# Softmax denominators in a transformer block: which engine sums the last two key tiles

## The chip, the core and the metric

The kernel runs on one core of a Trainium2 chip. The metric is the device time of one execution in microseconds (us). A core has five engines that run their own instruction lists in order and wait for each other by semaphores: TensorE (PE in the profile; its weight loads are PEld), VectorE (DVE), ScalarE (ACT), GpSimd (POOL) and SyncE (SP), which here issues DMA transfers. TensorE multiplies matrices held in the on-chip memory SBUF and leaves the results in PSUM, which has eight banks of 128 x 512 fp32.

## The reference

One block of a transformer, for one sequence of 2048 tokens of width 1024: a modulation from a vector c, layer norm, causal attention with 32 query heads and 8 key and value heads of width 32, an output product with a gate, layer norm again, and a routed low-rank layer. Cut to what matters here:

```python
mod = (_silu(L0_c) @ L0_wmod).reshape(L0_c.shape[0], 6, 1, -1)
...
h = _layernorm(x, axis=-1) * (1 + ca) + sa
q = (x @ Wq).reshape(b, t, N_HEADS, HEAD_DIM).transpose(0, 2, 1, 3)
...
q = _apply_rope(q, cos, sin)
k = _apply_rope(k, cos, sin)
scores = jnp.einsum('bhqd,bhkd->bhqk', q, k_h) / math.sqrt(HEAD_DIM)
causal = jnp.triu(jnp.ones((t, t), dtype=bool), k=1)
scores = jnp.where(causal[None, None], jnp.finfo(scores.dtype).min, scores)
attn = jax.nn.softmax(scores, axis=-1)
ctx = jnp.einsum('bhqk,bhkd->bhqd', attn, v_h)
...
x = x + ga * _L0_attn_ref(h, L0_attn_Wq, L0_attn_Wk, L0_attn_Wv, L0_attn_Wo)
h = _layernorm(x, axis=-1) * (1 + cb) + sb
x = x + gb * _L0_ffn_ref(h, L0_ffn_route_w, L0_ffn_A, L0_ffn_Bw)
```

The softmax needs, for every query and head, the sum over all keys of the exponentials of the scores. These sums are the denominators of the title.

## The kernel before

**Steps and tiles.** Attention is cut into 32 steps, four blocks of 512 queries times eight groups of four heads. A step in block qb has 4 (qb + 1) key tiles of 128 keys: 4, 8, 12 and 16. For one key tile, `weights` (L1472) computes the scores of four heads, 128 keys by 512 queries each, into four PSUM banks, and ScalarE writes their exponentials into a buffer `et` of 128 x 4 x 512 fp32. The row maxima that are subtracted are found beforehand by separate products (`maxima_units`, L1402), reduced on VectorE, cast on GpSimd (`split_maxima`, L1437 to L1447) and turned by TensorE into rows (`shift_rows`, L1449). Of the last four tiles of each step the mask removes queries: tile nk - 2 holds only the last 256 of the 512 queries, tile nk - 1 only the last 128 (`offset`, L1469).

**What is done with a tile of exponentials.** `weighted_sum` (L1503) multiplies it with the values on TensorE, into one bank for the step. `accumulate` (L1516) adds it on GpSimd to an SBUF buffer `acc` of the same shape: tile 1 starts it as the sum of tiles 0 and 1, and tiles 2 to nk - 3 follow. The last two tiles are left out of `acc`. `denominators` (L1528) then sums over the keys by products with a matrix of ones: first `acc`, 512 queries wide, then the last two tiles, 256 and 128 wide, all into one bank `pd`. ScalarE copies it to `rd`, VectorE inverts it in four pieces (`invert`), and GpSimd multiplies the step's output by it (`divide`, L1545). In the last step VectorE does the adds in place of GpSimd.

**Buffers.** There are four `et` buffers and one `acc`. An `et` is free when TensorE's product with the values and its add, or for the last two tiles the product with ones, are done. The next step's first add can start once the product with ones has read `acc`.

**Order.** All instructions are issued in an order that `plan_order` (L97) finds at build time. It searches over small units: maxima (M), scores (S), weighted sums with their adds (P), denominators (D), the shift rows (R), pieces of the projections and of the output product (F), and the tail of each token tile (T). It keeps a model of when each engine, bank and buffer will be free, with a cost per unit written by hand; `sums` (L235) holds the model of the adds and `shares` (L258) that of the denominators. The best order is then issued as it stands (L1614 to L1645). So when the model's costs change, the whole order changes. A denominators unit may be chosen once all weighted sums of its step are issued (L346), and the next step's add of tile 1 only after it (L344).

**Two more users of GpSimd.** `rotary` (L834) applies the position rotation of queries and keys, partly on GpSimd (L844, L845), with a table `cs` that is loaded for each projection into a single buffer (L825, L826, issued on SyncE) and has one half multiplied by a sign on ScalarE (L832). The output product adds its gated result to the residual on GpSimd (L1112).

Of the kernel before, what the change touches and what calls it, by code (L numbers as in the profile page):

```python
# [25 lines left out]
QB = 512  # L26
# [51 lines left out]
TO_ENGINE, TO_PE, BETWEEN = 0.25, 0.2, 0.15  # L78
# [18 lines left out]
def plan_order(parts, trail, steps, ahead, starts, tiles, ends, rates, gates):  # L97
# [36 lines left out]
    last_step = len(steps) - 1  # L134
# [4 lines left out]
    def start(s, form, ready):  # L139

        old = s[FORM]
        if form == "Rb":
            price = 0.145 if old != "R" else 0.03
            form = "R"
        elif form == "R":
            price = 0.225 if old != "R" else 0.03
        elif form == "C":
            price = 0.11 if old == "R" else 0.16 if old == "W" else 0.02
        else:
            price = 0.11 if old == "R" else 0.16 if old == "C" else 0.06  # L150
        s[FORM] = form
        at = s[PE] + price
        return ready if ready > at else at

    def use(s, engine, us, after):
        t = s[engine]
        t = (after if after > t else t) + us
        s[engine] = t
        return t + 0.09

    def take(s, n):

        s[GOT] = tuple(bank for _, bank in s[FREE][:n])
        ready, s[FREE] = s[FREE][n - 1][0], s[FREE][n:]
        return ready

    def give(s, *banks):
        s[FREE] = tuple(sorted(s[FREE] + banks))

    def free_et(s, at, n):  # L170
        s[ETS] = s[ETS] + (at + BETWEEN,) * n

    def flush(s):
        while s[LATER]:
            divide(s)
# [56 lines left out]
    def et_ready(s, i):  # L232
        return s[READY][i - s[SCORED] + 4]

    def sums(s):  # L235
        i = s[SUMMED]
        n, kc = tiles[i]
        nk = 4 * (steps[n][0] + 1)
        width = QB - max(0, kc * P - steps[n][0] * QB)
        ready = et_ready(s, i)  # L240
        at = ready + TO_PE
        if kc == 0:
            at = max(at, take(s, 1))
            s[SUM_BANK] = s[GOT][0]
        s[PE] = start(s, "C", at) + 0.00167 * width
        s[WORK] += 0.00167 * width
        if kc == nk - 1:
            give(s, (use(s, ACT, 0.5, s[PE] + TO_ENGINE) + TO_PE, s[SUM_BANK]))
        adder, us = (DVE, 0.0043) if n == last_step else (POOL, 0.00875)
        if kc == 1:  # L250
            s[ACC] = use(s, adder, us * QB, max(ready + BETWEEN, s[ACC_FREE]))
            free_et(s, max(s[ACC], s[PE]), 2)
        elif 1 < kc < nk - 2:
            s[ACC] = use(s, adder, us * width, ready + BETWEEN)
            free_et(s, max(s[ACC], s[PE]), 1)
        s[SUMMED] += 1

    def shares(s):  # L258
        flush(s)
        n = s[SHARED]  # L260
        ready = max(take(s, 1), s[ACC] + TO_PE, et_ready(s, ends[n] - 1) + TO_PE)
        s[PE] = start(s, "C", ready) + 0.00167 * (QB + 384)
        s[WORK] += 0.00167 * (QB + 384)
        s[ACC_FREE] = s[PE] + TO_ENGINE
        free_et(s, s[PE], 2)
        s[RD] = use(s, ACT, 0.5, s[PE] + TO_ENGINE)
        give(s, (s[RD] + TO_PE, s[GOT][0]))
        s[LATER] = 5
        s[SHARED] += 1
# [57 lines left out]
    def choices(s):  # L327
# [14 lines left out]
        if s[SUMMED] < s[SCORED]:  # L342
            n, kc = tiles[s[SUMMED]]
            if not (s[SHARED] < n and kc == 1) and s[FILL] >= sums_need[s[SUMMED] > 0]:  # L344
                found.append((et_ready(s, s[SUMMED]) + TO_PE, "P", sums))
        if s[SHARED] < last_step and s[SUMMED] >= ends[s[SHARED]]:  # L346
            found.append((max(one, s[ACC] + TO_PE), "D", shares))
# [25 lines left out]
    s = [0.0] * len(Plan.FIELDS)  # L373
# [24 lines left out]
    while key <= top:  # L398
# [13 lines left out]
        for _, s in sorted(kept.values(), key=lambda k: k[0])[:WIDTH]:  # L412
# [4 lines left out]
            if s[LATER] and s[DVE] < s[PE]:  # L417
                s = list(s)
                divide(s)
            while (  # L420
# [3 lines left out]
                s = list(s)  # L424
                follow(s)
            found = choices(s)
            if not found:

                if s[TRAIL] < s[KNOWN] and not KINDS[trail[s[TRAIL]]][0]:
                    n = tokens_for.get(s[TRAIL], 0)  # L430
                    if n > len(s[TOKENS]):
                        continue
                    s = list(s)
# [30 lines left out]
def adaln_block_kernel(  # L464
# [105 lines left out]
    class Stream:  # L570
        def __init__(self, pool, tag, depth):
            self.pool, self.tag, self.depth = pool, tag, depth
            self.loads, self.tiles = [], []
            self.freed = self.used = 0
# [9 lines left out]
        def take(self, n=1):  # L584
            got = self.tiles[self.used : self.used + n]
            assert len(got) == n
            self.used += n
            return got
# [78 lines left out]
    def bank(name):  # L667
        count[0] += 1
        return psum.tile([P, QB], F32, tag=f"b{chosen.pop(0)}", name=f"{name}_{count[0]}")
# [177 lines left out]
    class Project:  # L847
# [77 lines left out]
        def start(self):  # L925
            self.h_t = one.tile([P, NC, TB], F32, tag="h_t", name=f"h_t_{self.b}")
# [532 lines left out]
    class Attend:  # L1459
        def __init__(self, n):  # L1460
            self.n = n
            self.qb, self.m = steps[n]
            self.nk = 4 * (self.qb + 1)
            self.ets = {}

            last = n == len(steps) - 1
            self.adder = nc.vector if last else nc.gpsimd

        def offset(self, kc):  # L1469
# [46 lines left out]
        def accumulate(self, kc):  # L1516

            off, et = self.offset(kc), self.ets[kc]
            if kc == 1:
                self.acc = one.tile([P, 4, QB], F32, tag="acc", name=f"acc_{self.n}")  # L1520
                first = self.ets[0]
                if off:
                    self.adder.tensor_copy(self.acc[:, :, :off], first[:, :, :off])
                self.adder.tensor_add(self.acc[:, :, off:], first[:, :, off:], et[:, :, off:])  # L1524
            elif 1 < kc < self.nk - 2:
                self.adder.tensor_add(self.acc[:, :, off:], self.acc[:, :, off:], et[:, :, off:])  # L1526

        def denominators(self):  # L1528
            pd = bank(f"pd_{self.n}")
            parts = [(0, self.acc)]  # L1530
            parts += [(self.offset(kc), self.ets[kc]) for kc in (self.nk - 2, self.nk - 1)]
            for i, (off, et) in enumerate(parts):
                for j, rows in groups:
                    nc.tensor.matmul(  # L1534
                        pd[rows, off:], ones_p[:, :HD], et[:, j, off:],
                        start=(i == 0), stop=(i == 2),
                    )
            self.rd = one.tile([P, QB], F32, tag="rd", name=f"rd_{self.n}")
            nc.scalar.copy(self.rd, pd)  # L1539
# [28 lines left out]
    ends = [sum(s.nk for s in attend[: n + 1]) for n in range(len(steps))]  # L1568


    parts, phase_ends, costs, held = [], [0], [], {}
# [12 lines left out]
    for qb in range(NQB):  # L1584
        nk = 4 * (qb + 1)
# [28 lines left out]
    for letter, banks in order:  # L1614
# [8 lines left out]
        i = done_of[letter]  # L1623
        done_of[letter] += 1
        if letter == "M":
            units[i]()
            n = ahead[i][0]
            if i == final[n]:
                split_maxima(n)
        elif letter == "S":  # L1630
            n, kc = tiles[i]
            now[0] = n
            attend[n].weights(kc)
        elif letter == "P":
            n, kc = tiles[i]
# [68 lines left out]
```

## Time and profile before

The median of three runs is 1782.79 us (1782.09 to 1783.23). The profiled execution took 1782.16 us, of which 1780.4 us lie between its first and last instruction (the span); its granted TensorE clock averages 0.996 of full speed.

| stretch (us from the span's start) | TensorE busy | VectorE busy | ScalarE busy | GpSimd busy |
|---|---|---|---|---|
| 157 to 329 (denominators of steps 0 to 7) | 168.12 of 172 | 106.38 | 59.89 | 68.06 |
| 329 to 656 (to step 15) | 324.34 of 327 | 206.34 | 131.40 | 219.50 |
| 656 to 1163 (to step 23) | 503.22 of 507 | 310.25 | 218.00 | 374.47 |
| 1684 to 1780.4 (last step and the end) | 86.99 of 96.4 | 76.96 | 44.77 | 35.70 |

The costliest groups that the change concerns, by shape:

| line, engine | tile and width | count | busy us | mean ns |
|---|---|---|---|---|
| L1526 GpSimd add | acc, 2048 elements per partition | 157 | 713.3 | 4543 |
| L1526 GpSimd add | acc, 1536 elements | 23 | 79.5 | 3455 |
| L1524 GpSimd add | acc from tiles 0 and 1, 2048 elements | 23 | 104.4 | 4541 |
| L1534 TensorE product with ones | acc, 512 columns | 256 | 34.7 | 615 |
| L1534 TensorE product with ones | tile nk - 2, 256 columns | 256 | 20.2 | 387 |
| L1534 TensorE product with ones | tile nk - 1, 128 columns | 256 | 13.2 | 277 |

How to read it: a busy time is the time in which at least one instruction of the group ran. An fp32 product counts as two instructions, and the four heads' products run beside each other in the array and overlap, so their mean is not what one of them costs; that is read from the start of one group of products to the start of the next. GpSimd's and VectorE's instructions don't overlap with others of the same engine.

### The profile page before, as it was taken

To read this page: it belongs to the slowest core of one execution; us is meant where nothing else is said; L and a number is where in the kernel's file an instruction comes from. 1 tells how busy PE (TensorE), PEld (TensorE's weight loads), DVE (VectorE), ACT (ScalarE), POOL (GpSimd) and SP (SyncE) were. 2 spreads that over 40 slices of the span, in tenths; PEclk is the share of its full clock that TensorE was granted. 3 is DMA by queue.
4 is the path that set the end of the run, shared out by engine and by line. 5 is a ranking of instruction groups with operands and counts; after the bars stand their busy time and mean duration, and the time that the engine had idled before them with its cause. 6 is when DMAs were issued, how large, how long until landed. Compare 5 with 4: busy or idle time off the path is not lost.

```text
span 1780.4 us, 55951 instructions
## 1 busy us (share of the span) xinstructions
PE 1747.0 (98%) x25112; PEld 708.9 (40%) x25112; DVE 1094.3 (61%) x2160; ACT 740.0 (42%) x1634; POOL 1185.1 (67%) x568
## 2 busy tenths in 40 slices
PE   7999999999999999999999999999999999999997
PEld 3655555444444333334444343333333333333333
DVE  2455456755755674676475566575566765666497
ACT  1203334344433424455444333454544444455452
POOL 1233343487567649657885866978979778798852
PEclk9999999999999999999999999999999999999999
DMA  9512323212422421131103011101102111110101
GB/s 350 181 30 74 115 80 103 73 50 62 137 73 96 153 87 49 49 102 61 61 26 125 26 49 68 41 37 49 49 25 73 37 61 49 49 49 25 49 13 49
DMA packets 68496, 130.57 MB, mean 73 GB/s; under 512 B 3744, under 2 KB 20768, under 8 KB 68256
## 3 DMA queue, kind: packets, MB, share of 16 engines
q1 hardware_dynamic: 66928, 125.85, 20.5%
q8 instruction: 196, 3.21, 0.8%
q10 hardware_dynamic: 1328, 1.15, 0.2%
q14 instruction: 44, 0.36, 0.1%
HBM read 118.59 MB, written 8.39 MB: 71 GB/s over the span
## 4 chain that ended last, share of the span: by engine, by line
PE 88%; POOL 6%; DVE 2%; issue 2%; DMA 1%; ACT 1%; POOLq 0%; ACTq 0%; DVEq 0%
PE sm L1426 15%; PE po L1508 14%; PE sc L1492 12%; PE pw L675 11%; PE pq L966 11%; PE sc L1479 5%; POOL acc L1526 5%; PE pd L1534 3%; PE pk L675 3%; PE pv L675 2%; PE pa L675 2%; PE open L966 2%; PE pf L675 2%; PE sm L1419 1%; DVE mx L1432 1%
## 5 line engine op out<-in xcount | busy, mean ns | idle before, releaser
L1432 DVE TENSOR_REDUCE mx<-sm 128x1 f32<-128x512 f32 (+3 forms) x1280 | 689.0, 602 | 397.7 <-PE sm L1426 396.2
L1498 ACT ACTIVATE et<-sc 128x512 f32<-128x512 f32 (+3 forms) x1280 | 578.4, 540 | 705.5 <-PE sc L1492 701.3
L1526 POOL TENSOR_TENSOR acc<-acc,et 128x2048 f32<-128x2048 f32 (+1 forms) x180 | 792.8, 4404 | 31.8 <-ACT et L1498 22.8
L1426 PE MATMUL sm<-k_t,q 32*128 32x512 f32 (+3 forms) x3328 | 336.6, 475 | 3.0 <-ACT et L1498 3.0
L1492 PE MATMUL sc<-q,k_t 32*128 32x512 f32 (+3 forms) x2560 | 297.2, 536 | 0.0
L1508 PE MATMUL po<-et,v_sb 128*32 128x512 f32 (+3 forms) x2560 | 294.8, 538 | 0.1
L675 PE MATMUL pw<-w,q 128*32 128x512 f32 x1920 | 238.7, 598 | 0.0
L1524 POOL TENSOR_TENSOR acc<-et,et 128x2048 f32<-128x2048 f32 (+1 forms) x31 | 132.1, 4261 | 98.5 <-ACT et L1498 83.1
L966 PE MATMUL pq<-h_t,w 128*32 128x256 f32 x3072 | 191.9, 384 | 0.0
L1426 PEld LDWEIGHTS sm<-k_t,q 32*128 32x128 f32 x3328 | 139.5, 184 | 116.9 <-issue 43.5
L966 PEld LDWEIGHTS pq<-h_t,w 128*32 128x32 f32 x3072 | 90.5, 110 | 100.6 <-issue 44.8
L1508 PEld LDWEIGHTS po<-et,v_sb 128*32 128x32 f32 x2560 | 59.0, 108 | 175.5 <-issue 152.3
L1543 DVE RECIPROCAL rd<-rd 128x128 f32<-128x128 f32 x128 | 112.4, 919 | 18.9 <-ACT rd L1539 18.8
L1479 PE MATMUL sc<-nt,ones_h 32*128 32x512 bf16 (+3 forms) x1280 | 120.1, 352 | 3.5 <-ACT rd L1539 2.9
L1112 POOL TENSOR_TENSOR x<-ag,x 128x512 f32<-128x512 f32 x40 | 60.9, 1523 | 87.3 <-DVE ag L1111 87.3
L1492 PEld LDWEIGHTS sc<-q,k_t 32*128 32x128 f32 x2560 | 115.5, 185 | 5.8 <-issue 2.1
L1479 PEld LDWEIGHTS <-ones_h 32*128 32x128 bf16 x1280 | 32.9, 91 | 207.6 <-issue 201.5
L844 POOL TENSOR_TENSOR swap_q<-swap_q,cs 128x512 f32<-128x512 f32 x32 | 40.9, 1277 | 105.7 <-DVE swap_q L841 105.7
L675 PEld LDWEIGHTS pw<-w,q 128*32 128x32 f32 x1920 | 50.1, 109 | 129.3 <-issue 110.8
L1547 POOL TENSOR_TENSOR q<-q,rd 128x512 f32<-128x512 f32 x31 | 41.6, 1343 | 67.3 <-DVE rd L1543 49.5
L1111 DVE TENSOR_TENSOR ag<-pw,gate 128x512 f32<-128x512 f32 x40 | 27.5, 687 | 62.5 <-PE pw L675 60.9
L844 POOL TENSOR_TENSOR swap_k<-swap_k,cs 128x512 f32<-128x512 f32 x8 | 10.2, 1276 | 82.7 <-DVE swap_k L841 82.7
(146 smaller groups left out, 1340.0 us busy)
## 6 DMA issues: line engine op xcount, KB each, us to landing
w<-in_wo_dram SPq DMA_DIRECT2D x112, 256.0 KB
w<-in_wmod_dram SPq DMA_DIRECT2D x48, 512.0 KB
w<-in_wq_dram SPq DMA_DIRECT2D x48, 512.0 KB
x<-in_x_dram SPq DMA_DIRECT2D x32, 512.0 KB
out_dram<-x SPq DMA_DIRECT2D x16, 512.0 KB
w<-in_wv_dram SPq DMA_DIRECT2D x12, 512.0 KB
w<-in_wk_dram SPq DMA_DIRECT2D x12, 512.0 KB
wq<-in_wq_dram SPq DMA_DIRECT2D x8, 512.0 KB
```

Source lines behind the costliest of these rows:

```text
L675: nc.tensor.matmul(dst[rows], left[:, rows], right, start=start, stop=stop)
L966: nc.tensor.matmul(ps[j * HD : (j + 1) * HD, a * TB : (a + 1) * TB], self.query_weights(half, k, j * P + h * HD), self.h_t[:, k, :], start ...
L1112: nc.gpsimd.tensor_add(x1[t][:, cols], tmp, x1[t][:, cols])
L1426: nc.tensor.matmul(ps[j][:, a:b], q[rows, t * P : (t + 1) * P], k[rows, kc * QB + a : kc * QB + b], start=not masked, stop=(a, b) == spans ...
L1432: nc.vector.tensor_reduce(mx[:, t, j : j + 1, kc], ps[j][:, :nk], AX.X, ALU.max)
L1479: nc.tensor.matmul(ps[j][:, off:], ones_h[rows, :], nt[rows, off:], start=True, stop=False,)
L1492: nc.tensor.matmul(ps[j][:, off:], k[rows, kc * P : (kc + 1) * P], q[rows, off:], start=False, stop=True,)
L1498: nc.scalar.activation(et[:, j, off:], ps[j][:, off:], AF.Exp, scale=1.0 / math.sqrt(HD))
L1508: nc.tensor.matmul(self.po[rows, off:], v_sb[:, kc, 4 * (self.m // 4) + j, :], et[:, j, off:], start=(kc == 0), stop=(kc == self.nk - 1),)
L1524: self.adder.tensor_add(self.acc[:, :, off:], first[:, :, off:], et[:, :, off:])
L1526: self.adder.tensor_add(self.acc[:, :, off:], self.acc[:, :, off:], et[:, :, off:])
L1543: nc.vector.reciprocal(part, part)
```

## The change

The adder takes the last two tiles as well in all steps but the last, and the product with ones has one part instead of three there. The last step, in which VectorE adds, keeps its three parts. The planner's model is changed in the same way: `sums` counts an add for every tile from 2 on and frees the tile's buffer when it is done, and `shares` waits for the adder alone, costs 512 columns instead of 896 and no longer frees two buffers.

```diff
-        elif 1 < kc < nk - 2:
+        elif 1 < kc < (nk - 2 if n == last_step else nk):
             s[ACC] = use(s, adder, us * width, ready + BETWEEN)
             free_et(s, max(s[ACC], s[PE]), 1)
...
-        ready = max(take(s, 1), s[ACC] + TO_PE, et_ready(s, ends[n] - 1) + TO_PE)
-        s[PE] = start(s, "C", ready) + 0.00167 * (QB + 384)
-        s[WORK] += 0.00167 * (QB + 384)
+        s[PE] = start(s, "C", max(take(s, 1), s[ACC] + TO_PE)) + 0.00167 * QB
+        s[WORK] += 0.00167 * QB
         s[ACC_FREE] = s[PE] + TO_ENGINE
-        free_et(s, s[PE], 2)
...
             last = n == len(steps) - 1
+
+            self.apart = 2 if last else 0
             self.adder = nc.vector if last else nc.gpsimd
...
-            elif 1 < kc < self.nk - 2:
+            elif 1 < kc < self.nk - self.apart:
                 self.adder.tensor_add(self.acc[:, :, off:], self.acc[:, :, off:], et[:, :, off:])
...
             parts = [(0, self.acc)]
-            parts += [(self.offset(kc), self.ets[kc]) for kc in (self.nk - 2, self.nk - 1)]
+            apart = range(self.nk - self.apart, self.nk)
+            parts += [(self.offset(kc), self.ets[kc]) for kc in apart]
             for i, (off, et) in enumerate(parts):
                 for j, rows in groups:
                     nc.tensor.matmul(
                         pd[rows, off:], ones_p[:, :HD], et[:, j, off:],
-                        start=(i == 0), stop=(i == 2),
+                        start=(i == 0), stop=(i == self.apart),
                     )
```

The order of the whole program is planned anew with these costs.

## The prediction

> **What bounds the kernel now.** I read the page's busy shares first, then what TensorE waited for, then the last full block, then single step ends.
>
> ```profile
> PE 1747.0 (98%) x25112; PEld 708.9 (40%) x25112; DVE 1094.3 (61%) x2160; ACT 740.0 (42%) x1634; POOL 1185.1 (67%) x568
> PE 88%; POOL 6%; DVE 2%; issue 2%; DMA 1%; ACT 1%; POOLq 0%; ACTq 0%; DVEq 0%
> ...
> PE mr L781 <- DVE sign L557: 8.9, 1, 8.9
> PE mc L793 <- DVE rows L787: 5.1, 6, 1.4
> PE sm L1426 <- ACT et L1498: 3.0, 1, 3.0
> PE sc L1479 <- ACT rd L1539: 2.9, 1, 2.9
> PE pwh L1174 <- DVE wh L1166: 2.8, 1, 2.8
> ...
> core 0: us, PE busy (x) PEld busy (x) DVE busy (x) ACT busy (x) POOL busy (x), PEclk, DMA share, GB/s
> 1163.00:1684.00 521.00, 519.81 (x6140) 177.34 (x6132) 330.41 (x636) 250.29 (x534) 443.95 (x152) 1.00 0.13 46
> ```
>
> TensorE is busy 1747.0 of 1780.4 us, and the chain of waits is 88% TensorE. What it waits for (us in total, times, longest) is nearly all at the two ends of the run; between 329 and 1733 us its waits come to 6.7 us, of which the 3.0 is the largest. The last row is the stretch from the denominators of step 23 to those of step 30, seven steps: TensorE 519.81 of 521 us, GpSimd 443.95. So work taken from TensorE shortens the run, as long as GpSimd, which is second there at 85%, can take its share without making TensorE wait. The 6% of GpSimd in the chain is no wait of that size: the chain runs through its adds between 1331 and 1373 us, for instance, where TensorE shows no idle time.
>
> **What is removed.** In 31 of 32 steps the denominators' product loses two parts, 256 and 128 columns wide for four heads; the last step keeps them.
>
> ```profile
> 1605.34 3.45 POOL L1526 TENSOR_TENSOR acc<-acc,et 128x1536 f32<-128x1536 f32 x1
> 1605.86 0.79 ACT L1498 ACTIVATE et<-sc 128x128 f32<-128x128 f32 x4 [3.77 <-PE sc L1492]
> 1608.73 1.27 POOL L1112 TENSOR_TENSOR x<-ag,x 128x512 f32<-128x512 f32 x1
> 1612.18 1.07 PE L1534 MATMUL pd<-acc,ones_p 128*32 128x512 f32 x8
> 1613.06 0.83 PE L1534 MATMUL pd<-et,ones_p 128*32 128x256 f32 x16
> 1613.83 0.39 PE L1479 MATMUL sc<-nt,ones_h 32*128 32x512 bf16 x4
> 1617.38 4.54 POOL L1524 TENSOR_TENSOR acc<-et,et 128x2048 f32<-128x2048 f32 x1 [7.37 <-ACT et L1498]
> ```
>
> These rows are the end of step 29 (start, duration). The products of 512 columns hold TensorE from 1612.18 to 1613.06, 0.88 us (0.86 in other steps); the 384 columns that go are three quarters of that, 0.65, and the next work starts 0.77 later, which includes a change to products by rows that stays. 31 x 0.65 = 20.2 us. By columns and form, the rest of TensorE's work is the same list; in the new order it changes form 1750 times, in the old 1749.
>
> **What is added.** Two GpSimd adds a step, of 1024 and 512 elements per partition. The trace has 2048 at 4.54 us, 1536 at 3.455 and a 512 multiply (L1547) at 1.27, so 2.12 ns per element: 2.37 + 1.29 = 3.66 us a step, 113 us in all. GpSimd goes from 1185 to 1298 us, 73%. They lie beside TensorE, so they cost nothing while something covers them. The cover is in the rows above: after the add of tile 13 and a residual add, GpSimd stands idle for 7.37 us until tile 1 of the next step is there. Both new adds fit, as their tiles are written (tile 15 at 1606.65): they end near 1613.7. The product with ones would come 1.7 us later than it did, and the first add of step 30 would hardly move. In the seven steps these idle times before a step's first add are 33.1 us, the added work 7 x 3.66 = 25.6.
>
> The rule that speaks against this is in the Trainium skill, GPSIMD Engine Reference, Engine selection: elementwise adds belong on VectorE, GpSimd being about half as fast. The rows agree (2.69 us against 4.54 for the same add), and by that rule 113 us are paid for 20. The row that decides is the idle time: 77 us of the 521 are free there, and TensorE has none. I take the row; cost nothing. Nor does GpSimd slow VectorE here: its 2048 adds before the last step stay within 4.53 to 4.58 us.
>
> **What waits for what.** The product with ones now waits for an add of the last tile instead of the last exponentials. TensorE runs in order, so behind a late product with ones stand the next scores and projections, and behind those ScalarE's exponentials. In the trace the product starts 0.1 to 17.6 us after the step's last add, 4.2 in the median, under 1.4 in five of 31 steps. In the new order, counting products at these rates, it stands 2.6 to 23.6 us of TensorE work behind the step's last score tile, and 7.9 to 17.0 in steps 24 to 30. Even if GpSimd has then still to add tiles 13, 14 and 15, it needs 0.9 + 3.46 + 2.37 + 1.29 = 8.0 us. So in most steps the wait is covered, by tenths in some. One place is not: in step 10 GpSimd starts the adds of tiles 2 to 7 only after step 11's casts (L1447), 3 x 4.6 + 3.46 + 2.37 + 1.29 = 20.9 us, and TensorE gets to the product about 18 us after the casts. I put 2.9 us there and 1.5 us for the steps with tenths. The tiles' buffers come free at these adds; by the same count three of 300 score tiles would find theirs late, by at most 1.6 us, which the tenths cover.
>
> What a wait costs is shown at 960 us, where TensorE is idle for the 3.0 us listed above:
>
> ```profile
> 960.00:964.00 4.00, 1.00 (x6) 0.52 (x4) 1.29 (x2) 1.17 (x5) 1.97 (x6) 0.81 0.78 249
> 964.00:966.00 2.00, 2.00 (x12) 0.48 (x13) 0.41 (x1) 0.00 (x0) 0.00 (x0) 0.50 0.39 158
> 966.00:968.00 2.00, 2.00 (x20) 0.65 (x16) 0.88 (x2) 0.59 (x1) 0.00 (x0) 0.50 0.04 8
> 968.00:970.00 2.00, 2.00 (x26) 0.73 (x16) 0.00 (x0) 0.59 (x1) 0.00 (x0) 0.67 0.00 0
> ```
>
> The seventh column is the granted clock: half speed from 963.5 to 968, then 0.67, so another 2.3 + 0.6 = 2.9 us are lost; the wait costs 5.9. The skill (TensorE: Matmul & The Clock Gate, the HAM clock gate) puts the fall at an idle window of about 3.4 us and the recovery at as much busy time. By the page a 2.9 us wait costs only itself, by the row 5.8. I take the row: 5.8 + 1.5 = 7.3 us of new waits; the ends are 0 and about 25 (four such waits).
>
> The old 3.0 us wait has a cause that the new order moves: the rotation table's buffer came free late, since its last reader on GpSimd stood behind four adds (from 945.5 to 958.2), so the table's load (issued on SP at 959.5) and ScalarE's sign multiply (962.76) were late, and the exponentials behind it. TensorE has 9.6 us of work in the old order between that projection's last product and the next score tile behind the multiply, 18.7 in the new. I count it as gone: -5.9; if it stays, 0. Other loads stand in SP's queue in equal number, and TensorE waited 0.2 us for one in the whole run. The reciprocals and the division start with the product, at most a few us later; no output waited for them.
>
> **Sum.** The profiled execution took 1782.16 us: 1782.2 - 20.2 - 5.9 + 7.3 = 1763.4. The median of the runs is 0.6 us higher, within their spread of 1.1, so I say 1763.5.
>
> **Rivals.** (1) GpSimd sets the pace in the last block, the other side. Before, a step there takes 521 / 7 = 74.4 us and GpSimd's work 63.4, with 11.0 idle. If that idle time is a fixed price of the handover (product, its read, the next tile) and not cover, GpSimd's cycle becomes 63.4 + 3.66 + 11.0 = 78.1, TensorE's 73.8: 7 x 4.3 = 30 us lost, 1782.2 - 20.2 + 30 = **1792**. It decides for a slower kernel once more than 9.6 of the 11.0 us stay. For it: 85% busy, the 9s of its row in the slices. Against it: most of that idle time is waiting for exponentials of tiles that the adds can overlap. 4%.
> (2) Half of this: some 9 of the 11.0 us stay, or four to six waits at step ends each draw half clock: 10 to 20 us back, **about 1775**. 10%.
> (3) The waits don't show and the old one goes: 1782.2 - 20.2 - 5.9 = **1756**. 8%.
> (4) The change doesn't do what it says, because the planner's new order loses elsewhere what the products gave: **about 1782**, within 0.2%, 3.6 us, about what a measurement can tell from no change. The equal count of changes of form is against it. 3%.
> The forecast, 1758 to 1769, has 75%.
>
> **Range and chances.** 1757 to 1770 leaves most of (1), (2) and (4) out and half of (3). Faster by over 0.2%: the forecast, (3), and nearly all of (2), 0.92; the same 0.04; slower 0.04.
>
> **What would show it.** TensorE's busy time about 20 us less, its share still 97 to 98%; two rows of GpSimd adds, 31 each, at 2.37 and 1.29 us, and its total near 1298; the times before a step's first add on GpSimd shorter by 3 to 4 us; no 3.0 us wait with half clock near 950; a short TensorE wait for the adder at the end of step 10. Wrong would be: waits of TensorE for the adder of over 10 us in all, granted clock below 1 in the middle of the run, or a busy time that falls by much less than 20.

## The result

The changed kernel takes 1768.4 us, the median of six runs (1766.8 to 1770.5), against 1782.4 us for the kernel before in the same six rounds (1779.5 to 1783.6). The ratio is 0.9923, with a 95% interval of 0.991 to 0.9936: 14.0 us less, where 18.9 were forecast, inside the stated range. The profiled execution took 1769.27 us, its span is 1767.5 us. Of all runs told of below one is left out of its median, the fourth with all casts on VectorE, which took 2083.9 us at a granted clock of 0.829.

The page of the changed kernel, busy time of each engine:

```profile
PE 1733.2 (98%) x24616; PEld 692.6 (39%) x24616; DVE 1093.5 (62%) x2160; ACT 740.7 (42%) x1634; POOL 1298.4 (73%) x630
```

The groups of GpSimd's adds, by shape (line, tile, shapes, count, busy us, mean ns, and the idle time before them with what ended it):

```profile
L1526 POOL TENSOR_TENSOR acc<-acc,et 128x1024 f32<-128x1024 f32 x31 | 73.2, 2362 | 2.0 <-ACT et L1498 0.5
L1526 POOL TENSOR_TENSOR acc<-acc,et 128x512 f32<-128x512 f32 x31 | 39.4, 1272 | 6.8 <-ACT et L1498 4.6
```

What TensorE waited for between 329 and 1725 us (us in total, times, longest). The lines of the helpers have moved up by two: L1452 is the product of the shift rows, L673 the output product, L1535 the product with ones.

```profile
PE nt L1452 <- POOL nb L1445: 3.6, 4, 2.3
PE pw L673 <- DMA w<-in_wo_dram: 2.2, 2, 1.5
PE sm L1417 <- ACT et L1498: 1.1, 3, 0.6
...
PE pd L1535 <- POOL acc L1526: 0.2, 1, 0.2
```

The reader is to see three things. The removed work is gone (496 records fewer, 16 a step), yet TensorE's busy time fell by 13.8 us only. GpSimd took exactly the predicted load: 113 us more, at 2.36 and 1.27 us an add. And TensorE hardly waits for the adder at the product with ones: 0.2 us, once. The old 3.0 us wait near 960 us is gone too, but there are waits for casts and for weights that the kernel before did not have in this size (its longest wait for casts was 0.6 us, for these weights it had none). Two of the signs that the prediction had named for being wrong did come: the busy time fell by much less than 20 us, and the granted clock is below 1 in the middle of the run, near 440 us.

### The profile page after: what moved, and what is told of

It reads as the page before. It is cut to its first block, busy times and chain, and to the rows that moved or that the text cites. A ratio compares the mean times of both kernels' runs of the same rounds, so it can differ in the third digit from the quotient of the medians.

```text
span 1767.5 us, 55092 instructions
## 1 busy us (share of the span) xinstructions
PE 1733.2 (98%) x24616; PEld 692.6 (39%) x24616; DVE 1093.5 (62%) x2160; ACT 740.7 (42%) x1634; POOL 1298.4 (73%) x630
## 4 chain that ended last, share of the span: by engine, by line
PE 83%; POOL 10%; DVE 2%; issue 2%; DMA 1%; ACT 1%; SPq 0%; POOLq 0%; ACTq 0%; DVEq 0%
PE sm L1424 14%; PE po L1508 12%; PE sc L1492 12%; PE pq L964 11%; PE pw L673 10%; POOL acc L1526 8%; PE sc L1479 5%; PE pk L673 3%; PE pv L673 3%; PE pd L1535 2%; PE open L964 2%; PE pf L673 1%; PE sm L1417 1%; PE pa L673 1%; PE mr L779 1%
## 5 line engine op out<-in xcount | busy, mean ns | idle before, releaser
L1526 POOL TENSOR_TENSOR acc<-acc,et 128x2048 f32<-128x2048 f32 (+1 forms) x242 | 905.0, 3740 | 30.6 <-ACT et L1498 17.8
L673 PE MATMUL pw<-w,q 128*32 128x512 f32 x1920 | 238.5, 598 | 2.4 <-DMA w<-in_wo_dram 2.2
L673 PEld LDWEIGHTS pw<-w,q 128*32 128x32 f32 x1920 | 49.4, 109 | 136.3 <-issue 111.3
L842 POOL TENSOR_TENSOR swap_k<-swap_k,cs 128x512 f32<-128x512 f32 x8 | 10.2, 1270 | 86.1 <-DVE swap_k L839 86.1
```

The source lines that it names most:

```text
L673: nc.tensor.matmul(dst[rows], left[:, rows], right, start=start, stop=stop)
```

## The experiments

A change of this kind has two halves that the planner ties together: other instructions, and another order for all instructions. The first experiments part them. Theory G was that GpSimd's longer queue gave back what is missing; theory O, that the new order has waits of its own.

**The new order with the old instructions.** In the changed kernel, only this line is undone, so that the last two tiles are summed by products again while the planner still believes in the change:

```diff
-            self.apart = 2 if last else 0
+            self.apart = 2
```

> The order planned for the change, with the instructions of before (the last two tiles are summed by products with ones again, GpSimd adds as before). Theory G (the change gave back about 7 us through GpSimd's longer queue): the 20 us of products come back, the losses at step 10 (late exponential buffers, half clock, about 5 us) go: 1783 to 1785 us, no half clock near 445 us. Theory O (the losses belong to the new order itself, whatever GpSimd does): 1768.4 + 20 = 1788 us or more, with the waits near 632 to 644 us still there. Both: the 3.0 us wait near 960 us stays away, since the order moved the rotation table's load.

Measured: 1783.8 us (1780.9 to 1787.2), ratio 1.0004 (0.9995 to 1.0012) to the kernel before. The order alone is worth nothing. In its profile no wait near 960 us is left, as predicted, but the two largest of the new waits are there, with the same sizes as in the changed kernel (waits of TensorE, as above):

```profile
PE nt L1452 <- POOL nb L1445: 3.7, 4, 2.3
PE pw L673 <- DMA w<-in_wo_dram: 2.3, 2, 1.5
```

So these are the order's and not GpSimd's adds'; that is theory O. The time itself fell in the range of theory G, since taking the products back cost 15.4 us and not the 20 that theory O had added.

The waits are not what makes this order cost as much as it saves. These rows are of the kernel before and of the order alone, between 60 and 1720 us (stretch, its length, busy times of TensorE, weight loads, VectorE, ScalarE and GpSimd, granted clock, DMA share, GB/s):

```profile
60.00:1720.00 1660.00, 1648.48 (x23756) 660.55 (x23752) 1030.91 (x2007) 704.81 (x1556) 1157.07 (x526) 1.00 0.19 64
60.00:1720.00 1660.00, 1648.32 (x23756) 657.78 (x23752) 1030.39 (x2005) 707.77 (x1558) 1159.19 (x526) 1.00 0.19 64
```

TensorE is idle for 11.5 us in the one and 11.7 in the other: the new waits only take the place of the old ones. Half clock became rarer: the profile before has 10.2 us of it in this stretch (3.4 from 184.2 us on, 6.8 from 962.5 on), the order alone has none, and over the runs the granted clock is 0.995 in the median of 15 before and 0.998 in that of 12 with the order alone. By 0.3% of 1780 us the new order should have been some 5 us faster (an estimate). It was not, so the same list of products took about 5 us more of TensorE's time in the new order. Which sequences of products cost that is not shown.

**The old order with the new instructions.** The kernel before with the changed `accumulate` and `denominators`, the planner untouched:

```diff
+            self.apart = 2 if last else 0
...
-            elif 1 < kc < self.nk - 2:
+            elif 1 < kc < self.nk - self.apart:
...
-            parts += [(self.offset(kc), self.ets[kc]) for kc in (self.nk - 2, self.nk - 1)]
+            parts += [(self.offset(kc), self.ets[kc]) for kc in range(self.nk - self.apart, self.nk)]
...
```

> The order of before, with the instructions of the change. If the new adds fit into GpSimd's idle time in the old order too, the full 20 us show: 1762 us. Theory W (the old order has too little TensorE work between a step's last score tile and the product with ones): the product waits for the adder in some ten steps, each for 1 to 4 us, the longer ones with half clock behind them: 1770 to 1785 us, and the waits are listed at the product with ones.

Measured: 1819.4 us, ratio 1.0207 (1.019 to 1.0224), 36 us slower than before and further out than theory W's 1785. Its busy row, then TensorE's waits:

```profile
PE 1741.9 (96%) x24616; PEld 695.5 (38%) x24616; DVE 1094.4 (60%) x2160; ACT 740.3 (41%) x1634; POOL 1296.0 (71%) x630
```

```profile
PE pd L1535 <- POOL acc L1527: 34.2, 17, 5.9
```

17 of the 31 products with ones wait for the adder, 34.2 us in all, and the mean granted clock of the core is 0.989 instead of 0.996. Without the 20.2 us of products, TensorE's busy time should be near 1727; it is 1741.9, about 15 us more. The lower clock accounts for some 13 of them (an estimate: 1.1% of 1814.5 us against 0.4% of 1780.4). The change is faster only because the planner was told of it.

**Neither products nor adds.** In the new order, the last two tiles are left out of the denominators:

```diff
-            elif 1 < kc < self.nk - self.apart:
+            elif 1 < kc < self.nk - 2:
...
-            nc.scalar.copy(self.rd, pd)
+            nc.scalar.activation(self.rd, pd, AF.Identity, bias=ones_p[:, 0:1])
```

> The order planned for the change, in which the last two tiles are summed by nobody (in 31 steps the denominators lack them; ScalarE adds 1 to each denominator in the copy that it makes anyway). It splits the 15.4 us between the order with the instructions of before (1783.8) and the change (1768.4) into the products' worth and the adds' cost. Theory S (the products are worth 31 x 0.65 = 20.2 us and the adds cost the rest): 1763.5 us, no half clock near 440 us. Rival V (the products are worth only some 15 us and the adds nothing): 1768 us.

Measured: 1767.3 us (1763.7 to 1769.5), ratio 0.9911 (0.9893 to 0.9929). That is nearer to rival V: in this order, taking the products out saves 16.5 us, and the adds that replace them cost 1 to 2 us. By the intervals of the ratios each of these differences is known only to within some 4 us, so the cost of the adds is not clear of noise. Since the order is the same in all three kernels, the times from one product with ones to the next can be compared place by place in the profiles:

| from the order with old instructions | to neither | from neither to the change |
|---|---|---|
| 20 of 33 stretches, each | -0.6 to -0.7 | 0.0 to 0.3 |
| step 5 to 6 | -0.6 | +0.5 |
| step 6 to 7 | +0.1 | -0.2 |
| step 9 to 10 | -0.6 | +3.2 (+1.6 in a second profile) |
| step 14 to 15 | +1.3 | -2.0 (-0.1 in the second) |
| all, with nine others | -16.2 | +2.8 (+2.1) |

In most stretches the step gets shorter by just the predicted 0.65 us. In the sum 3.9 us are missing. Of these, 1.9 lie between steps 14 and 15: TensorE waits there for the casts and the weights, 4.5 to 5.0 us in every profile of this order, and behind that wait 3.4 us at half clock follow in the kernel with neither and in the second profile of the change, none in the other two. Between steps 6 and 7 it is 0.7 us, where TensorE waits too; the rest lies in stretches in which TensorE is hardly idle, and is not explained.

**The changed kernel again**, for step 10.

> The changed kernel once more, unaltered, for its spread and for a second look at step 10. The order alone, with the instructions of before, has the same wait there (1.0 us against 1.5) without half clock. Theory H (half clock follows a short wait only in some executions): the profile shows half clock near 440 to 447 us or not, and the times spread by 3 to 4 us. Theory G (GpSimd's longer queue makes it each time): half clock at the same place. 1766 to 1771 us.

Measured: 1768.0 us (1766.6 to 1770.2). The profiles below show the same few products in the same order, with the columns as above. First the order with the old instructions, where the place lies some 5 us later:

```profile
441.00:445.00 4.00, 3.00 (x48) 1.63 (x47) 3.93 (x10) 2.14 (x5) 3.92 (x2) 1.00 1.05 358
445.00:449.20 4.20, 4.20 (x48) 2.22 (x44) 3.64 (x10) 1.72 (x7) 1.84 (x1) 1.00 0.06 18
```

Then the changed kernel's first profile:

```profile
436.00:440.00 4.00, 2.51 (x48) 1.36 (x40) 3.67 (x8) 1.90 (x4) 3.92 (x2) 0.97 0.99 334
440.00:447.20 7.20, 7.20 (x44) 3.51 (x44) 4.71 (x13) 1.79 (x8) 5.18 (x3) 0.54 0.06 20
```

And its second:

```profile
436.00:440.00 4.00, 2.50 (x46) 1.55 (x39) 3.61 (x9) 2.47 (x8) 3.92 (x2) 1.00 0.97 336
440.00:447.20 7.20, 7.20 (x56) 2.58 (x59) 4.53 (x13) 2.73 (x6) 5.31 (x4) 0.76 0.05 16
```

The kernel with neither products nor adds passes the same place too:

```profile
435.40:439.40 4.00, 2.49 (x48) 1.36 (x40) 3.70 (x8) 1.85 (x4) 3.92 (x2) 1.00 0.98 337
439.40:443.40 4.00, 4.00 (x40) 2.12 (x40) 3.34 (x9) 1.52 (x7) 1.62 (x1) 1.00 0.03 10
```

TensorE is idle for 1.0, 1.5, 1.5 and 1.5 us. What follows differs: full clock, 0.54 over 7.2 us, 0.76 over 7.2 us, and full clock again. With the same idle time of 1.5 us there is half clock for 6.8 us, for 3.4 us or not at all, so neither the length of the wait nor the new adds decide it; it comes in some executions, as theory H had it. The wait is not the one at the product with ones that I had predicted for this step. ScalarE waits there for an exponential buffer that GpSimd has yet to add from:

```profile
438.00 0.17 PE L1417 MATMUL sm<-pick,later 32*128 32x32 bf16 x1 [0.62 <-DVE mx L1430]
438.10 2.06 ACT L1498 ACTIVATE et<-sc 128x512 f32<-128x512 f32 x4 [2.20 <-POOL acc L1526]
438.75 0.19 PE L1417 MATMUL sm<-pick,later 32*128 32x32 bf16 x2 [0.58 <-ACT et L1498]
```

These rows of the changed kernel (start, duration, idle time before and what ended it) show GpSimd's late add of tile 4 holding the exponentials, these holding the score banks, and those TensorE. That add is an old one, and the kernel without the new adds has the wait as well.

The predicted wait was there, but hidden. In the second profile GpSimd's last add of step 10 ends at 444.7 us and the product with ones starts at 445.0, after 3.4 us at half clock that cost TensorE 1.7. At full clock TensorE would have come at about 443.3 and waited 1.4 us for the adder (an estimate from these figures). So here the half clock and the wait for the adder stand in each other's place.

**The adds twice**, first in the unchanged order, then with the planner told:

```diff
-                self.adder.tensor_add(self.acc[:, :, off:], self.acc[:, :, off:], et[:, :, off:])
+                for _ in range(2 if kc >= self.nk - 2 else 1):
+                    self.adder.tensor_add(self.acc[:, :, off:], self.acc[:, :, off:], et[:, :, off:])
```

> The change with its two new adds made twice, in the same order (the denominators then count the last two tiles twice). Theory U (the new order has used up GpSimd's slack): the product with ones starts 0.1 to 24.8 us after the last add in the changed kernel, under 3.66 us in 22 of 31 steps; what is missing there sums to 45 us: 1810 to 1850 us. Rival C (more idle time of GpSimd can still be filled): under 1780 us.

```diff
-            s[ACC] = use(s, adder, us * width, ready + BETWEEN)
+            s[ACC] = use(s, adder, us * width * (2 if kc >= nk - 2 else 1), ready + BETWEEN)
```

> The two new adds made twice, as in the earlier run, but now the planner is told of their double length, so the order is planned for it. Theory P (the cover comes from the order: TensorE has 73.7 us of work a step in the last block, GpSimd would have 70.7): most of the 61 us that the doubling cost in the unchanged order come back, 1770 to 1785 us. Rival Q (GpSimd is full with any order): over 1805 us.

Measured: 1829.7 us unplanned, 1789.3 us planned (ratio to before 1.0041, 1.0027 to 1.0056). TensorE's waits at the product with ones over the whole run, unplanned:

```profile
PE pd L1536 <- POOL acc L1527: 46.9, 22, 5.0
```

and planned:

```profile
PE pd L1536 <- POOL acc L1527: 10.4, 11, 2.4
```

The missing margins, 45 us in 22 steps, were within some 2 us of the waits that came, in 22 steps, so the margin between the last add and the product with ones tells how long TensorE waits when GpSimd gets more to do. In the changed kernel it is 2.2 us in the median (4.2 before) and under 1.4 us in nine steps (five before). The rest of the 61 us that the doubling cost is mostly TensorE's busy time, 1748.5 us instead of 1733.2, at a granted clock of 0.988 instead of 0.997. A new order takes back 40 of the 61 us, so neither theory P's range nor rival Q is right: the order can cover much, but with twice the added work the change no longer pays here.

**Other orders for the same change.** Three edits touch only the planner: its cost of an add, its time between weight loads, and how many candidates its search keeps. A fourth gives the last two tiles to VectorE, planned as well.

```diff
-        adder, us = (DVE, 0.0043) if n == last_step else (POOL, 0.00875)
+        adder, us = (DVE, 0.0043) if n == last_step else (POOL, 0.00899)
```

> The change with the planner's cost of a GpSimd add raised from 0.00875 to 0.00899 us per column (4.48 to 4.60 us for 512, the pitch that the trace shows). Theory G (late adds give 7 us back because the planner thinks GpSimd is quicker than it is): half clock at step 10 goes, margins before the products with ones grow by 1 to 2 us, 1760 to 1765 us. Theory O (the losses are luck of an order): anything from 1760 to 1775 us, without relation to the margins.

```diff
-            s[QUEUE] = max(s[QUEUE], s[PE] + 0.3) + 1.5
+            s[QUEUE] = max(s[QUEUE], s[PE] + 0.3) + 3.0
```

> The change with the planner's time between two weight loads raised from 1.5 to 3.0 us, nothing else. In the changed kernel the products of the output waited 2.2 us for their weights near 640 us, and 4.6 us with the other add cost. Theory O (what the change lost beyond the products lies in what the new order gets wrong): those waits go, 1762 to 1767 us. If not: within 2 us of 1768.4, or another order with other waits, up to 1775 us.

```diff
-        adder, us = (DVE, 0.0043) if n == last_step else (POOL, 0.00875)
+        adder, us = (DVE, 0.0043) if n == last_step or kc >= nk - 2 else (POOL, 0.00875)
...
-                self.adder.tensor_add(self.acc[:, :, off:], self.acc[:, :, off:], et[:, :, off:])
+                adder = nc.vector if kc >= self.nk - 2 else self.adder
+                adder.tensor_add(self.acc[:, :, off:], self.acc[:, :, off:], et[:, :, off:])
```

> The last two tiles are added by VectorE instead of GpSimd, planned for it. GpSimd's busy time returns to about 1185 us, VectorE's rises by some 31 x 2.0 = 62 us to 1156 us. Theory G (GpSimd's load gives back part of the 20 us): 1761 to 1765 us. Theory O (the order's own waits do): 1765 to 1775 us with small waits at other places. If VectorE's adds hold up the maxima: over 1775 us, with TensorE waiting for VectorE.

```diff
-    WIDTH, GRAIN = 200, 0.4
+    WIDTH, GRAIN = 400, 0.4
```

> The change, with twice as many candidates kept in the planner's search (400 instead of 200), so another order again with the same costs and the same instructions. Five orders with these products so far gave 1768 to 1779 us (the doubled adds left out). Theory O (the time beyond the products' work is a matter of which order the search happens upon, by some 10 us): anything from 1762 to 1779 us, and not the 1762 us or less that a better search would give if the model were true. Rival: the wider search finds fewer waits, under 1763 us.

| kernel | median us | ratio to before (95%) |
|---|---|---|
| the change | 1768.4 | 0.9923 (0.991 to 0.9936) |
| add cost 0.00899 | 1774.5 | 0.9954 (0.9939 to 0.9969) |
| slower loads | 1778.8 | 0.9978 (0.997 to 0.9985) |
| VectorE adds the last two | 1776.0 | 0.9965 (0.9952 to 0.9978) |
| wider search | 1759.5 | 0.9871 (0.9855 to 0.9888) |

Of four orders with the same instructions, the one of the change among them, the slowest takes 19 us more than the fastest; that is more than the change itself is worth. (The last expectation speaks of five orders tried until then; with the one of VectorE there were four.) Mending one cost did not mend the time: with the true length of an add, step 10 is quiet, but the output product waits 4.6 us for weights; with slower loads assumed, it still waits 2.0 us for them and 6.4 us for the adder. All that was expected of the slower loads was missed, by 4 us at the nearest. With the true add cost theory O's wide range held and theory G's did not. The adds on VectorE came out 1 us above theory O's range, with waits of 6.8 us for ScalarE's copy of a denominator and 3.3 us for the maxima; the number is that of the third case (over 1775 us), but TensorE's waits for VectorE are only a part, and theory G's 1761 to 1765 us did not come.

The wider search, on the contrary, went below what theory O allowed it, and its rival's guess of under 1763 was right. It is the fastest version found, 1.3% under the kernel before. Its busy row has fallen by 20.5 us, from 1747.0 to 1726.5, but that is not the products alone: some 5 us of it are the half clock of the kernel before between 60 and 1720 us, of which nothing is left here:

```profile
PE 1726.5 (98%) x24616; PEld 692.0 (39%) x24616; DVE 1092.5 (62%) x2160; ACT 740.2 (42%) x1634; POOL 1295.0 (74%) x630
```

and its largest waits in the middle of the run:

```profile
PE pd L1535 <- POOL acc L1526: 3.2, 3, 2.0
PE nt L1452 <- POOL nb L1445: 1.4, 2, 1.0
```

No wait for these weights is left, and nowhere from 60 to 1720 us does the clock fall. Whether a still wider search gains more was not tried. Nor was the wider search given the old instructions, so how much of the 1.3% needs the change is not known.

**The casts on VectorE**, for step 11 alone and for all steps, in the order of the change. The five lines of `split_maxima` go from `nc.gpsimd` to `nc.vector`:

```diff
-        nc.gpsimd.tensor_copy(nb[:, :, :, 0], neg)
-        nc.gpsimd.tensor_sub(rest, neg, nb[:, :, :, 0])
+        engine = nc.vector if n == 11 else nc.gpsimd
+        engine.tensor_copy(nb[:, :, :, 0], neg)
+        engine.tensor_sub(rest, neg, nb[:, :, :, 0])
...
```

> The change with the five small casts and subtractions of step 11 on VectorE; everything else and the order unchanged. At step 10 they stand in GpSimd's queue before the adds of tiles 2 to 7 and wait for VectorE, so the adds start at 424.3 instead of 423.0 us. Theory K (the wait near 438 us is for the buffer of tile 4, and it brings the half clock): the add of tile 4 ends 1.4 us earlier, TensorE's idle time there falls from 1.5 us to under 0.5, half clock goes: 1763 to 1766 us. If half clock has another cause: 1767 to 1768 us.

> The change with all 32 groups of casts and subtractions on VectorE, the order unchanged. GpSimd loses 39 us of busy time and its adds no longer stand behind casts that wait for VectorE; the shift rows' products wait for VectorE's own results. Theory K: the waits for the casts (3.6 us) and the half clock at step 10 fall away or shrink: 1760 to 1765 us. Rival: VectorE runs 1.1 us longer before each group of maxima, and the score banks come free later: 1768 us or more.

Measured: 1775.6 us with one group moved, 1932.4 us with all. Theory K's numbers fell both times. The second expectation's rival had the direction right (1768 us or more), but neither expectation named the mechanism. Rows of the kernel with step 11's casts moved (start, duration):

```profile
423.35 0.20 DVE L1442 CAST nb<-neg 128x16 bf16<-128x16 f32 x1
423.39 9.13 POOL L1527 TENSOR_TENSOR acc<-acc,et 128x2048 f32<-128x2048 f32 x2
423.59 4.37 DVE L1443 TENSOR_TENSOR rest<-neg,nb 128x16 f32<-128x16 f32 x1
...
428.23 4.33 DVE L1445 TENSOR_TENSOR rest<-rest,nb 128x16 f32<-128x16 f32 x1
```

Two subtractions of 16 elements take 4.37 and 4.33 us on VectorE, each until the GpSimd add that runs beside it ends (the two adds take 9.13 us from 423.39 on, so they end near 427.96 and 432.52; the subtractions end at 427.96 and 432.56), and the maxima behind them come 8 us late. So theory K could not be tested this way: GpSimd's adds did start 0.9 us sooner, but TensorE then waited 7.8 us for VectorE. The kernel with neither products nor adds tells against its second half: the same wait for tile 4's buffer, and no half clock.

## Why the prediction held, and where it did not

- **What bounds the kernel** was right: TensorE. GpSimd carries the extra 113 us at 73%, and no rival in which it sets the pace came true. The nearest to it is the old order with the new instructions, where it cost some 54 us (34.1 us more span, and 20.2 us of products gone): the place that the prediction named, the product with ones, with half clock behind the waits. It was avoided by the order, as the prediction's count of the work ahead of that product said.
- **The removed products**, 20.2 us: right per step (0.65 in most stretches), too high as a sum. 16.5 us showed in this order; 1.7 us of what is missing is half clock that the profile with neither has and the one with the order alone has not, so at full clock it would be about 18. The prediction took every step's saving as whole, and did not ask where TensorE would stand waiting in the new order.
- **The added adds**, no cost of their own: right in size, 2.36 + 1.27 us against 2.37 + 1.29, and nearly right in cost. The cover was in part another one than the prediction had read: GpSimd's idle time before a step's first add is 33.1 us over the seven late steps before, 22.8 in the new order with the old instructions and 17.0 with the change, so the adds took 5.8 us of it and the other 19.8 of their 25.6 went into idle time elsewhere. And that GpSimd does not slow VectorE did not follow from the length of GpSimd's own adds; VectorE's busy time shows it, 1094.3 us before and 1093.5 after.
- **New waits**, 7.3 us: too high. The change takes 1.1 us longer than the kernel with neither products nor adds, 2.1 by the ratios. At step 10 the product with ones would have had to wait, for half of what was forecast; TensorE came late enough by half clock behind another wait, which is there without the new adds too. That no wait shows at that product is chance.
- **The wait that goes**, -5.9 us: it went, and its half clock with it, and yet this is the term that failed, since the order as a whole is worth +0.2 us with the old instructions. The waits of other kinds that came (for step 15's casts 2.3 us, for the output's weights 2.2) only fill the place of the old ones. What used up the saving is that the same products take about 5 us more of TensorE's time in the new order. The prediction had taken that as nil, because the list of products is the same and changes of form are as many (1750 against 1749); this count doesn't show what an order costs. It is the part of rival (4) that did happen.

With the measured terms, 1782.4 + 0.2 - 16.5 + 1.1 = 1767.2, against 1768.4. This is no test, as the terms are differences between the same runs; what is left is the 1.1 us by which the kernel before differed between the rounds. Against the forecast the three terms that were off are off by +3.7, -6.2 and +6.1 us. The last two all but cancel, so that the forecast of 1763.5 came so close is in part luck.

What stays open is why one order costs TensorE 5 us more than another, and why TensorE falls to half clock behind a wait of 1.5 us in one execution and not in another. On the second, the Trainium skill (TensorE: Matmul & The Clock Gate, the HAM clock gate) speaks of an activity window of about 3.4 us that runs freely. Half clock of 3.4 and 6.8 us behind one and the same wait, or none, would fit a window that lies differently against the wait each time, but no run here tested it.

## What to carry to other kernels

When a planner orders the program, measure a change twice: with its order and the old instructions, and with its instructions and the old order. Here the first is worth nothing, the second costs 36 us, and together they gain 14. Work moved to an engine with idle time is nearly free as long as its result is due later than that engine needs; read that margin at the consumer, step by step, before moving more. And a count of what an order contains does not tell its time: four orders of one program differed by 19 us here, and a search with more candidates gained 9 us over the change.

## What was not expected of the hardware

A VectorE instruction with two inputs in SBUF lasted as long as the GpSimd add that ran at the time, though it was small: 16 elements took 4.37 us. With all groups moved, the shortest of such subtractions took 0.184 us, the medians were 2.37 us (first) and 0.185 us (second), and the longest took 4.55 us; a cast of 16 elements also took up to 4.46 us. The Trainium skill (Advanced Engine Details and Errata, GPSIMD Details) says that the two engines share an interface and conflict for such instructions; the rows agree, and in them the small one waits until the large one is done. In the last step of the kernel before, GpSimd's small adds beside VectorE's large ones show the reverse, 3.27 us instead of 1.27.

Half clock came behind idle times of 3.0 us (the kernel before) and of 1.5 us in three pieces (the changed kernel, both profiles), which is less than the skill's window of about 3.4 us would suggest; behind the same 1.5 us it did not come in the kernel with neither products nor adds. In every profile here each stretch at half clock between 60 and 1720 us lasts 3.4 us or a multiple of it.
